# Attention projections on four column strips, with two copies moved from VectorE in a four-layer transformer kernel

## The chip, the cores and the metric

The kernel runs on one core of a Trainium2 chip. The metric is the device time of one execution in microseconds, the median of several runs. The engines of the core are named as the profile names them: PE (TensorE), PEld (TensorE's weight loads), DVE (VectorE), ACT (ScalarE), POOL (GpSimd) and SP (SyncE, which issues the transfers).

## What is computed

Sixteen sequences of 256 tokens with 256 features pass through four layers; all data is fp32. Attention has 16 heads of 16 features.

- Layer 0: norm and modulation by a condition vector, masked self attention with rotary turning of q and k, a gated residual; then cross attention to 77 context tokens with a gated residual; then an MLP (256 to 1024 to 256) with a gated residual.
- Layer 1: cross attention with biases, plain residual.
- Layer 2: self attention with biases and a gated residual, cross attention with a plain residual, MLP with a gated residual.
- Layer 3: self attention and cross attention, both with rotary turning, plain residuals; MLP.

For one attention the reference is, in short:

```
xn = norm(x) * (1 + scale) + shift
q, k, v = xn @ Wq, src @ Wk, src @ Wv        # src is xn, or the context
q, k = rope(q), rope(k)                      # layers 0 (self only) and 3
x = x + gate * (softmax(q k^T / 4 [+ mask]) v @ Wo)
```

## The kernel before

Everything stays in the core's memory: `x_sb` holds all sixteen sequences. Each batch element's attention or MLP is cut into steps. The function `add` notes a step: its engine, an assumed duration, what it depends on, which buffers it takes (`Hold`), and a priority. `Order.solve` then goes through the steps with those durations and writes the order in which every engine gets its instructions; the engines run their lists in that order and wait for each other by semaphores. The eight PSUM banks (tag `b`) are handed from step to step. Within layers 1 and 2 and within each attention stage, steps of many batch elements are interleaved; the three MLP stages stand between (roughly 630 to 860, 1612 to 1850 and 2400 to 2630 us).

PE works in several divisions of its 128 x 128 array:

- full: contraction over 128 rows (or 77, the context length) and more than 32 output columns. The projections (`project_T` L619, `rotate_tasks` L671, `mmv` L787), the output projection in `residual` (L992), the transposes (L711, L606, L498) and the MLP (L1035, L992).
- row-tiled: four groups of 32 rows side by side, each with one pair of heads: scores for the maximum (L828, L840) and scores for the exponential (L922).
- four column strips of 32: the step `values` (L945), which multiplies the exponentials by v. For each of two heads it issues four matmuls, for PSUM partitions 0, 32, 64 and 96.
- 64 x 64: the mask of layer 0, in bf16 (L915).

The planner knows them as a `kind` of step ("row", "col", or none for full) and adds a turning time of 0.2 us (0.13 for "col") where the kind changes.

An attention runs so: `norm_tasks` normalises x (POOL `xn` L491) and turns it by a DVE transpose and two transfers through DRAM (`yd`, `xr`) into `xT`, scaled by ACT (L539). The projections follow. `take_q` (ACT) writes q into `kq`. `take_k` writes k twice into `kz`, slot 0 with every other group of 16 features set to zero and slot 1 with the others (the factors are in `par`): slot 0 is ACT's (L640, L642) and slot 1 is DVE's (L644, L646). Where there is rotary turning, DVE multiplies by the tables (L683, L686), POOL adds (L691), PE transposes back (L711), and `take_q` and `take_k` read that. Scores are made, DVE takes the maxima (L854 with the mask in layer 0's self attention, L858, L862), the maxima go through DRAM back into `kq`, scores are made again with them, ACT takes exponentials into `ec` (L936, L934), `values` multiplies with v, DVE transposes (`ts` L954) and takes reciprocals (L961), POOL multiplies (`od` L967), and DVE transposes into `oT` (L971). Then `residual` multiplies by the output weights. Without a gate DVE adds the product to x (L998). With one, DVE multiplies the PSUM product by the gate `gb` into `tmp` (L1005) and POOL adds `tmp` to x (L1008).

Of the kernel before, what the change touches and what calls it, by code (L numbers as in the profile page):

```python
# [13 lines left out]
ALU = mybir.AluOpType  # L14
AX = mybir.AxisListType

B, N, D, H, HD, LC, FF = 16, 256, 256, 16, 16, 77, 1024
P = 128
# [176 lines left out]
def pixart_kernel(ctx: ExitStack, tc: tile.TileContext, x, cond_t, ctx_in, mask_c, mask_s, tables, vecs, rows,  # L195
# [28 lines left out]
    def buf(h, tag=None):  # L224

        return pools[tag or h.tag][h.no]
# [385 lines left out]
        return s, last, hc  # L612


    def project_T(dst, w, xT):

        for g in range(NC):
            for k in range(NC):
                nc.tensor.matmul(dst[:, g, :], lhsT=w[:, k, g * P:(g + 1) * P], rhs=xT[:, k, :],  # L619
                                 start=(k == 0), stop=(k == NC - 1))  # L620
# [11 lines left out]

    def take_k(s, bias, n, src, a, use, prio):

        def one(i):
            kz, sc = s["kz"], par[:, i:i + 1]
            for g in ([slice(0, NC)] if bias is None else [0, 1]):
                bi = None if bias is None else kbias[bias][:, i, g:g + 1]
                if i == 0 and bias is None:
                    nc.scalar.activation(kz[:, i], src(), AF.Copy, scale=sc)  # L640
                elif i == 0:
                    nc.scalar.activation(kz[:, i, g, :], src()[:, g, :], AF.Identity, scale=sc, bias=bi)  # L642
                elif bias is None:
                    nc.vector.tensor_scalar_mul(kz[:, i], src(), sc)  # L644
                else:
                    nc.vector.tensor_scalar(kz[:, i, g, :], src()[:, g, :], sc, bi, ALU.mult, ALU.add)  # L646
        big = n == N
        d = (0.6 if big else 0.33) if bias is None else (0.95 if big else 0.5)
        return join([add("ACT", d, lambda: one(0), deps=[a], use=use, prio=prio),
                     add("DVE", d, lambda: one(1), deps=[a], use=use, prio=prio)], prio)  # L650

    def rotate_tasks(s, key, ws, xT, src_t, n, half, uses, name, prio):


        nt = (n + P - 1) // P
        r = min(n, P)
        width = len(ws) * D
        out_t, hold = [], []
        for group in ([list(range(nt))] if len(ws) == 1 else [[t] for t in range(nt)]):
            hm, hr, hq, u = Hold("b"), Hold("rope"), Hold("qk"), {}  # L660
            nm = f"{key}_{name}_{group[0]}"
            w_all = len(group) * width

            def mm(group=group, u=u, hm=hm, hq=hq):
                u["p"] = psum(hm)
                u["r1"] = s[key, group[0]] = buf(hq)
                for i, t in enumerate(group):
                    for j, w in enumerate(ws):
                        at = (i * len(ws) + j) * D
                        for k in range(NC):  # L670
                            nc.tensor.matmul(u["p"][0:r, at:at + D], lhsT=xT()[:, k, t * P:t * P + r],  # L671
                                             rhs=w()[:, k, :], start=(k == 0), stop=(k == NC - 1))

            def turns(group=group, u=u, hr=hr):
                r1 = u["r1"]
                r2 = u["r2"] = buf(hr)
                hn = width // HD
                for i, t in enumerate(group):
                    tt = (t * P % half) // P
                    pv, v1, v2 = (a[0:r, i * width:(i + 1) * width].rearrange("q (h w) -> q h w", w=HD)  # L680
                                  for a in (u["p"], r1, r2))
                    cs = tabT[0:r, tt, 0, :].unsqueeze(1).to_broadcast([r, hn, HD])
                    nc.vector.tensor_tensor(v1, pv, cs, ALU.mult)  # L683
                    for z in range(2):
                        sn = tabT[0:r, tt, 1, 8 * z:8 * z + 8].unsqueeze(1).to_broadcast([r, hn, 8])
                        nc.vector.tensor_tensor(v2[:, :, 8 * z:8 * z + 8], pv[:, :, 8 - 8 * z:16 - 8 * z], sn,  # L686
                                                ALU.mult)

            def plus(u=u, w_all=w_all):
                r1 = u["r1"][0:r, 0:w_all]  # L690
                nc.gpsimd.tensor_tensor(r1, r1, u["r2"][0:r, 0:w_all], ALU.add)  # L691
            size = len(group) * len(ws)
            a = add("PE", size * NC * MM, mm, deps=[src_t], take=[hm, hq], use=uses, prio=prio)
            d = add("DVE", 0.75 * size, turns, deps=[a, tab_t], take=[hr], use=[hm, hq], prio=prio)
            out_t.append(add("POOL", 0.65 * size, plus, deps=[d], use=[hr, hq], prio=prio))
            hold.append(hq)
        return out_t, hold, nt, r
# [18 lines left out]
    def attention(b, name, n, wv, wkeys, h_w, w_t, eps, mod, half, biases, masked, pre_add, gate, prio, ctxs=None,  # L716
# [31 lines left out]
        if half is None:  # L748
# [6 lines left out]
            def mmk():  # L755
                p = psum(hm2)
                u["k"] = p[:, 0:NC * n].rearrange("p (c n) -> p c n", n=n)
                project_T(u["k"], wv[kk], src())
            a = add("PE", (4 * MM) if self_ else 1.0, mmk, deps=[*src_t, w_t[kk], late_t], take=[hm2], use=[h_kq, *h_src, *h_w],
                    prio=prio)  # L760
            k_t = take_k(s, bk, n, lambda: u["k"], a, [hm2, h_kq], prio)
            a = add("PE", 4 * MM, mmq, deps=[xT_t, w_t[kq], late_t], take=[hm1], use=[h_kq, hx, *h_w], prio=prio)
            q_t = take_q(s, bq, lambda: u["q"], a, [hm1, h_kq], prio)
        elif self_:
            info = rotate_tasks(s, "qk", [lambda: wv[kq], lambda: wv[kk]], lambda: s["xT"],
# [16 lines left out]
        def mmv():  # L782
            ps = uv["p"] = psum(hm3)
            xT = src()
            for t in range(nk):
                for k in range(NC):
                    nc.tensor.matmul(ps[0:rows_n, t * D:(t + 1) * D], lhsT=xT[:, k, t * P:t * P + rows_n],  # L787
                                     rhs=wv[kv][:, k, :], start=(k == 0), stop=(k == NC - 1))

        def take_v():  # L790
# [2 lines left out]
            pairs = pairs.rearrange("p t h (a w) -> p t h a w", w=HD)  # L793
            for t in range(nk):
                nc.scalar.copy(pairs[:, t, :, 0:4:3, :], pv[:, t].rearrange("p (h i) w -> p h i w", i=2))
        a = add("PE", nk * NC * MM, mmv, deps=[*src_t, w_t[kv]], take=[hm3], use=[h_v, *h_src, *h_w], prio=prio)
        v_t = add("ACT", 0.37 * nk, take_v, deps=[a, ones_t], use=[hm3, h_v], prio=prio)


# [90 lines left out]
        for g in range(NC):  # L890
            u5, avs, h_av, h_so = {}, [], Hold("b"), Hold("ts")
            for kc in range(nk):
                h_e, ex = Hold("ec"), []

                def open_e(g=g, kc=kc, h_e=h_e):
                    if g == 0 and kc == 0:
                        s["oT"] = buf(h_ot)
                    for r in range(4):
                        s["e", g, kc, r] = buf(h_e)[:, r]
                t_e = add("NO", 0.0, open_e, deps=[qx_t, v_t, barrier], take=[h_e] if g or kc else [h_e, h_ot],  # L900
                          prio=prio)
                for rp in (1, 0):
                    hs = [Hold("b"), Hold("b")]
# [66 lines left out]
            def back(g=g, u5=u5):  # L970
# [5 lines left out]


        residual(s, b, [*done, w_t[ko]], lambda k, t: s["oT"][:, k, t * P:(t + 1) * P], lambda: wv[ko], NC, [h_ot, *h_w], gate, nm,
                 prio)
        return exps  # L980


    def residual(s, b, deps, lhsT, w, nk, holds, gate, name, prio, after=None):
        hm, u = Hold("b"), {}
        xf = x_sb[:, b].rearrange("p t d -> p (t d)")
        ts = []
        for t in range(NT):
            def mm(t=t):
                if t == 0:
                    u["p"] = psum(hm, NT)  # L990
                for k in range(nk):
                    nc.tensor.matmul(u["p"][:, t, :], lhsT=lhsT(k, t), rhs=w()[:, k, :], start=(k == 0),  # L992
                                     stop=(k == nk - 1))
            ts.append(add("PE", nk * MM, mm, deps=[*deps, *ts], take=[hm] if t == 0 else [],
                          use=holds if t == 0 else [hm, *holds], prio=prio))
        if gate is None:
            def plus():
                nc.vector.tensor_tensor(x_sb[:, b], x_sb[:, b], u["p"], ALU.add)  # L998
            x_done[b] = add("DVE", 0.69, plus, deps=[*ts, x_done[b]], use=[hm], prio=prio)
            return  # L1000
        ht = Hold("tmp")

        def times():
            s["tmp"] = buf(ht)
            nc.vector.tensor_tensor(s["tmp"], u["p"], s["gb"][:, 0:1, :].to_broadcast([P, NT, D]), ALU.mult)  # L1005

        def plus():
            nc.gpsimd.tensor_tensor(xf, xf, s["tmp"].rearrange("p t d -> p (t d)"), ALU.add)  # L1008
        a = add("DVE", 0.69, times, deps=[*ts, s["gb_t"]], take=[ht], use=[hm, s["hg"]], prio=prio)
        x_done[b] = add("POOL", 1.3, plus, deps=[a, x_done[b]], use=[ht], prio=prio)  # L1010


    def mlp(b, name, wv, h_w, w_t, eps, mod, func, b1, pre_add, gate, prio, barrier, before):
# [343 lines left out]
```

## Time and profile before

| what | value |
|---|---|
| median of 3 runs | 2632.84 us (2628.79 to 2638.83) |
| the profiled execution | 2631.43 us, span 2629.7 us |
| mean granted TensorE clock | 0.995 |
| PE busy | 98% of the span, 21512 matmul records |
| DVE, ACT, POOL busy | 62%, 48%, 42% |
| DMA | 143.10 MB, mean 54 GB/s |

One fp32 matmul is two matmul records and two weight-load records. A record's own length comes from a model, and neighbours overlap, so the distance between starts is the better measure. "Line" is the line of the kernel before. In a group's line, out<-in with "32*128" gives the rows and columns of the weights. The idle time before a group is put down to what ended it.

### The profile page before, as it was taken

What the parts mean: (1) busy time and instruction counts of PE and PEld (TensorE: products, weight loads), DVE (VectorE), ACT (ScalarE), POOL (GpSimd) and SP (SyncE); (2) the same over time, 40 slices, a digit from 0 to 9 for tenths busy, and PEclk for the clock granted to TensorE, in tenths of its full rate; (3) what the DMA queues carried; (4) which work ended last, traced back from release to release, by engine and by line L of the source; (5) the groups of instructions that cost most, each with busy time, mean ns of one, the idle gap of its engine ahead of it and who ended that gap; (6) DMA issues with size and microseconds to landing.
All of it is one profiled execution on the core that took longest, in us unless ns stands there. A gap on an engine that the chain in (4) does not pass through costs nothing. (4 is left out here: it accounts for less than half of the span.)

```text
span 2629.7 us, 56144 instructions
## 1 busy us (share of the span) xinstructions
PE 2575.5 (98%) x21512; PEld 1813.2 (69%) x21512; DVE 1627.7 (62%) x4537; ACT 1255.4 (48%) x2511; POOL 1113.5 (42%) x1413
## 2 busy tenths in 40 slices
PE   8999999999999899999999999999999999999999
PEld 5555565666888666666666667888666666666888
DVE  7888886676131577777777775111888887885100
ACT  2444455664333456555556654322455555554322
POOL 5233333558452355233334656442333324657310
PEclk9999999999999899999999999999999999999999
DMA  5000101223321121111111113111100001122110
GB/s 171 30 27 29 34 25 39 73 80 101 100 78 54 40 70 54 48 55 40 39 40 38 61 62 114 64 54 45 35 28 30 28 24 37 50 66 71 56 57 29
DMA packets 159749, 143.10 MB, mean 54 GB/s; under 512 B 24648, under 2 KB 124216, under 8 KB 158712
## 3 DMA queue, kind: packets, MB, share of 16 engines
q1 hardware_dynamic: 159480, 139.51, 16.9%
q8 instruction: 169, 2.77, 0.4%
q14 instruction: 100, 0.82, 0.1%
HBM read 91.86 MB, written 47.61 MB: 53 GB/s over the span
## 5 line engine op out<-in xcount | busy, mean ns | idle before, releaser
L936 ACT ACTIVATE ec<-bank 128x512 f32<-128x512 f32 (+1 forms) x1152 | 608.5, 596 | 514.0 <-PE bank L828 260.7
L922 PE MATMUL bank<-kq 32*128 32x256 f32 (+1 forms) x5120 | 627.9, 395 | 4.8 <-DMA kq<-mrow 4.4
L491 POOL TENSOR_SCALAR xn<-x_sb,mv,rstd 128x256 f32<-128x256 f32 x320 | 451.1, 1464 | 108.4 <-DVE y L519 97.8
L922 PEld LDWEIGHTS bank<-kq 32*128 32x128 f32 (+1 forms) x5120 | 357.2, 167 | 172.8 <-issue 105.1
L828 PE MATMUL bank<-kq 32*128 32x512 f32 x1536 | 432.5, 633 | 2.4 <-ACT ec L936 2.4
L858 DVE TENSOR_REDUCE mx<-bank 128x2 f32<-128x512 f32 x544 | 341.6, 681 | 46.0 <-PE bank L828 43.7
L945 PE MATMUL bank<-ec,v 128*32 128x256 f32 (+1 forms) x5120 | 347.9, 385 | 5.8 <-ACT ec L936 3.6
L1040 ACT ACTIVATE ec<-bank,vec 128x256 f32<-128x256 f32 x384 | 159.7, 467 | 401.3 <-PE bank L1035 373.2
L1035 PE MATMUL bank<-xT,kq 128*128 128x256 f32 x1536 | 341.4, 379 | 0.0
L992 PE MATMUL bank<-kq,ec 128*128 128x256 f32 x1536 | 339.7, 379 | 0.0
L992 PEld LDWEIGHTS bank<-kq,ec 128*128 128x128 f32 x1536 | 291.5, 190 | 39.5
L1035 PEld LDWEIGHTS bank<-xT,kq 128*128 128x128 f32 x1536 | 290.5, 190 | 40.4 <-issue 1.6
L967 POOL TENSOR_TENSOR od<-ts,rec 128x128 f32<-128x128 f32 x448 | 170.1, 402 | 318.7 <-DVE rec L961 318.1
L519 DVE STREAM_TRANSPOSE y<-xn 128x512 f32<-128x512 f32 x158 | 110.9, 702 | 298.9 <-DMA yd<-y 257.6
L945 PEld LDWEIGHTS bank<-ec,v 128*32 128x32 f32 (+1 forms) x5120 | 137.2, 109 | 183.0 <-issue 75.5
L862 DVE TENSOR_REDUCE mx<-bank 128x4 f32<-128x308 f32 x512 | 211.9, 468 | 55.4 <-PE bank L922 25.3
L466 POOL TENSOR_SCALAR rstd<-mv 128x2 f32<-128x2 f32 x160 | 37.5, 235 | 423.8 <-DVE mv L461 347.7
L854 DVE CUSTOM_DVE_ANT_0 junk<-bank,ctx 128x256 f32<-128x256 f32 x448 | 188.8, 421 | 45.2 <-PE bank L828 12.2
L954 DVE STREAM_TRANSPOSE ts<-bank 128x512 f32<-128x512 f32 x224 | 158.3, 707 | 76.6 <-PE bank L945 69.1
L691 POOL TENSOR_TENSOR qk<-qk,rope 128x512 f32<-128x512 f32 (+1 forms) x96 | 112.9, 1178 | 194.4 <-DVE rope L686 151.3
L1008 POOL TENSOR_TENSOR x_sb<-x_sb,tmp 128x512 f32<-128x512 f32 x80 | 101.6, 1270 | 179.4 <-DVE tmp L1005 179.2
L840 PE MATMUL bank<-kq 32*128 32x154 f32 x2048 | 167.1, 308 | 1.5 <-DVE ts L954 0.5
(164 smaller groups left out, 3437.8 us busy)
## 6 DMA issues: line engine op xcount, KB each, us to landing
yd<-y SPq DMA_DIRECT2D x158, 256.0 KB
xr<-yd SPq DMA_DIRECT2D x158, 256.0 KB
kq<-in_mod_dram SPq DMA_DIRECT2D x10, 512.0 KB
cin<-in_ctx_in_dram SPq DMA_DIRECT2D x36, 128.0 KB
x_sb<-in_x_dram SPq DMA_DIRECT2D x16, 256.0 KB
gb<-gate_g0m SPq DMA_DIRECT2D x16, 256.0 KB
gb<-gate_g2a SPq DMA_DIRECT2D x16, 256.0 KB
gb<-gate_g2m SPq DMA_DIRECT2D x16, 256.0 KB
```

What stands on the lines that cost most here:

```text
L491: nc.gpsimd.tensor_scalar(to, of, s["mv"][:, t, 0:1], s["rstd"][:, t:t + 1], ALU.subtract, ALU.mult)
L828: ls.append(lambda ps=ps, R=R, keys=keys: nc.tensor.matmul(ps.rearrange("p (s k) -> p s k", k=N), lhsT=s["qx"][R, 0, g, t * P:(t + 1) * P] ...
L840: ls.append(lambda ps=ps, R=R, keys=keys, tt=tt: nc.tensor.matmul(ps[:, 2 * tt * n:2 * (tt + 1) * n].rearrange("p (s k) -> p s k", k=n), l ...
L854: nc.vector.tensor_tensor_reduce(junk, u[i][:, i2 * N:(i2 + 1) * N], mb[:, t, :], -1.0, 3.0e38, ALU.add, ALU.min, m[:, i2, g, t:t + 1])
L858: nc.vector.tensor_reduce(m[:, :, g, t], u[i].rearrange("p (s k) -> p s k", k=N), AX.X, ALU.max, negate=True)
L862: nc.vector.tensor_reduce(m[:, :, g].rearrange("p s t -> p t s"), u[i][:, 0:4 * n].rearrange("p (t s k) -> p t s k", s=2, k=n), AX.X, ALU. ...
L922: (lambda ps=u[i], R=R, q=q: nc.tensor.matmul(ps[0:rows_n, q * N:(q + 1) * N], lhsT=s["kz"][R, q, g, kc * P:kc * P + rows_n], rhs=s["qx"][ ...
L936: nc.scalar.activation(e, u[i][0:rows_n], AF.Exp)
L945: nc.tensor.matmul(u5["p"][32 * r:32 * r + 32, 1 - q, :], lhsT=s["v"][0:rows_n, kc, 8 * g + 2 * r + 1 - q, :], rhs=s["e", g, kc, r][0:rows ...
L967: nc.gpsimd.tensor_tensor(ov[:, :, HD * i:HD * i + HD], ts[:, i, :, HD * i:HD * i + HD], rec[:, i, :].unsqueeze(2).to_broadcast([P, N // 3 ...
L992: nc.tensor.matmul(u["p"][:, t, :], lhsT=lhsT(k, t), rhs=w()[:, k, :], start=(k == 0), stop=(k == nk - 1))
L1035: nc.tensor.matmul(u["p"][:, j, :], lhsT=wv["w1"][:, k, f * P:(f + 1) * P], rhs=s["xT"][:, k, :], start=(k == 0), stop=(k == NC - 1))
```

## The change

- A new function `strips` makes one 128-column product from four matmuls of 32 weight columns each, one for each quarter of the output's partitions, all with the same right-hand side. The self-attention projections and every q projection of 256 tokens use it, and so does the output projection of every attention (`nk == NC`). The k and v projections of the 77 context tokens, the transposes and the MLP stay as they were. The steps concerned are told to the planner as kind "col".
- In `take_k`, for 256 keys without bias (self attention of layers 0 and 3), slot 1 is also copied by ACT.
- In `residual`, for layer 0's self attention (`by_pool`), ACT copies the PSUM product into `tmp`, and POOL multiplies it by the gate and then adds it to x. The POOL step also keeps the gate buffer.
- Each step that opens an `ec` buffer also names the hold on `oT`; before, only the first did.

```diff
+    def strips(dst, pairs):
+        for k, (l, r) in enumerate(pairs):
+            for J in (slice(32 * j, 32 * j + 32) for j in range(4)):
+                nc.tensor.matmul(dst[J], lhsT=l[:, J], rhs=r, start=(k == 0), stop=(k == len(pairs) - 1))
+
+    def project_T(dst, w, xT, small=False):
         for g in range(NC):
+            if not small:
+                strips(dst[:, g, :], [(w[:, k, g * P:(g + 1) * P], xT[:, k, :]) for k in range(NC)])
+                continue
...
@@ take_k
-                if i == 0 and bias is None:
+                if bias is None and (i == 0 or big):
                     nc.scalar.activation(kz[:, i], src(), AF.Copy, scale=sc)
...
-                     add("DVE", d, lambda: one(1), deps=[a], use=use, prio=prio)], prio)
+                     add("ACT" if big and bias is None else "DVE", d, lambda: one(1), deps=[a], use=use, prio=prio)], prio)
@@ rotate_tasks
+                        if r == P:
+                            strips(u["p"][:, at:at + D], [(xT()[:, k, t * P:(t + 1) * P], w()[:, k, :]) for k in range(NC)])
+                            continue
...
-            a = add("PE", size * NC * MM, mm, deps=[src_t], take=[hm, hq], use=uses, prio=prio)
+            a = add("PE", size * NC * MM, mm, kind="col" if r == P else None, deps=[src_t], take=[hm, hq], use=uses, prio=prio)
@@ attention
-                project_T(u["k"], wv[kk], src())
+                project_T(u["k"], wv[kk], src(), not self_)
...
+                if self_:
+                    strips(ps[:, t * D:(t + 1) * D], [(xT[:, k, t * P:(t + 1) * P], wv[kv][:, k, :]) for k in range(NC)])
+                    continue
...
-                t_e = add("NO", 0.0, open_e, deps=[qx_t, v_t, barrier], take=[h_e] if g or kc else [h_e, h_ot],
+                t_e = add("NO", 0.0, open_e, deps=[qx_t, v_t, barrier], take=[h_e, h_ot],
@@ residual
+                if nk == NC:
+                    strips(u["p"][:, t, :], [(lhsT(k, t), w()[:, k, :]) for k in range(nk)])
+                    return
...
+            if by_pool:
+                nc.scalar.copy(s["tmp"], u["p"])
+            else:
+                nc.vector.tensor_tensor(s["tmp"], u["p"], s["gb"][:, 0:1, :].to_broadcast([P, NT, D]), ALU.mult)
...
+            if by_pool:
+                nc.gpsimd.tensor_tensor(s["tmp"], s["tmp"], s["gb"][:, 0:1, :].to_broadcast([P, NT, D]), ALU.mult)
             nc.gpsimd.tensor_tensor(xf, xf, s["tmp"].rearrange("p t d -> p (t d)"), ALU.add)
...
+        a = add("ACT" if by_pool else "DVE", 0.6 if by_pool else 0.69, times, deps=[*ts, s["gb_t"]], take=[ht],
+                use=[hm, s["hg"]], prio=prio)
+        x_done[b] = add("POOL", 2.6 if by_pool else 1.3, plus, deps=[a, x_done[b]], use=[ht, s["hg"]], prio=prio)
```

More of the change, by code (lines that the diff above doesn't have):

```diff
@@ L612, in context_T @@
         return s, last, hc
-    def project_T(dst, w, xT):
+    def strips(dst, pairs):
[3 more added lines that the diff above has]
+    def project_T(dst, w, xT, small=False):
         for g in range(NC):
+            if not small:
+                strips(dst[:, g, :], [(w[:, k, g * P:(g + 1) * P], xT[:, k, :]) for k in range(NC)])
+                continue
             for k in range(NC):
@@ L633, in take_k @@
     def take_k(s, bias, n, src, a, use, prio):
+        big = n == N
         def one(i):
@@ L646, in one @@
                     nc.vector.tensor_scalar(kz[:, i, g, :], src()[:, g, :], sc, bi, ALU.mult, ALU.add)
-        big = n == N
         d = (0.6 if big else 0.33) if bias is None else (0.95 if big else 0.5)
         return join([add("ACT", d, lambda: one(0), deps=[a], use=use, prio=prio),
-                     add("DVE", d, lambda: one(1), deps=[a], use=use, prio=prio)], prio)
+                     add("ACT" if big and bias is None else "DVE", d, lambda: one(1), deps=[a], use=use, prio=prio)], prio)
     def rotate_tasks(s, key, ws, xT, src_t, n, half, uses, name, prio):
@@ L757, in mmk @@
                 u["k"] = p[:, 0:NC * n].rearrange("p (c n) -> p c n", n=n)
-                project_T(u["k"], wv[kk], src())
-            a = add("PE", (4 * MM) if self_ else 1.0, mmk, deps=[*src_t, w_t[kk], late_t], take=[hm2], use=[h_kq, *h_src, *h_w],
+                project_T(u["k"], wv[kk], src(), not self_)
+            a = add("PE", (4 * MM) if self_ else 1.0, mmk, kind="col" if self_ else None, deps=[*src_t, w_t[kk], late_t], take=[hm2], use=[h_kq, *h_src, *h_w],
                     prio=prio)
             k_t = take_k(s, bk, n, lambda: u["k"], a, [hm2, h_kq], prio)
-            a = add("PE", 4 * MM, mmq, deps=[xT_t, w_t[kq], late_t], take=[hm1], use=[h_kq, hx, *h_w], prio=prio)
+            a = add("PE", 4 * MM, mmq, kind="col", deps=[xT_t, w_t[kq], late_t], take=[hm1], use=[h_kq, hx, *h_w], prio=prio)
             q_t = take_q(s, bq, lambda: u["q"], a, [hm1, h_kq], prio)
@@ L795, in take_v @@
                 nc.scalar.copy(pairs[:, t, :, 0:4:3, :], pv[:, t].rearrange("p (h i) w -> p h i w", i=2))
-        a = add("PE", nk * NC * MM, mmv, deps=[*src_t, w_t[kv]], take=[hm3], use=[h_v, *h_src, *h_w], prio=prio)
+        a = add("PE", nk * NC * MM, mmv, deps=[*src_t, w_t[kv]], take=[hm3], kind="col" if self_ else None, use=[h_v, *h_src, *h_w], prio=prio)
         v_t = add("ACT", 0.37 * nk, take_v, deps=[a, ones_t], use=[hm3, h_v], prio=prio)
@@ L895, in open_e @@
                 def open_e(g=g, kc=kc, h_e=h_e):
-                    if g == 0 and kc == 0:
-                        s["oT"] = buf(h_ot)
+                    s["oT"] = buf(h_ot)
                     for r in range(4):
                         s["e", g, kc, r] = buf(h_e)[:, r]
-                t_e = add("NO", 0.0, open_e, deps=[qx_t, v_t, barrier], take=[h_e] if g or kc else [h_e, h_ot],
+                t_e = add("NO", 0.0, open_e, deps=[qx_t, v_t, barrier], take=[h_e, h_ot],
                           prio=prio)
@@ L978, in attention, with residual @@
         residual(s, b, [*done, w_t[ko]], lambda k, t: s["oT"][:, k, t * P:(t + 1) * P], lambda: wv[ko], NC, [h_ot, *h_w], gate, nm,
-                 prio)
+                 prio, by_pool=masked and self_)
         return exps
-    def residual(s, b, deps, lhsT, w, nk, holds, gate, name, prio, after=None):
+    def residual(s, b, deps, lhsT, w, nk, holds, gate, name, prio, by_pool=False):
         hm, u = Hold("b"), {}
@@ L993, in mm @@
                                      stop=(k == nk - 1))
-            ts.append(add("PE", nk * MM, mm, deps=[*deps, *ts], take=[hm] if t == 0 else [],
+            ts.append(add("PE", nk * MM, mm, deps=[*deps, *ts], take=[hm] if t == 0 else [], kind="col" if nk == NC else None,
                           use=holds if t == 0 else [hm, *holds], prio=prio))
@@ L1004, in times @@
             s["tmp"] = buf(ht)
-            nc.vector.tensor_tensor(s["tmp"], u["p"], s["gb"][:, 0:1, :].to_broadcast([P, NT, D]), ALU.mult)
+            if by_pool:
+                nc.scalar.copy(s["tmp"], u["p"])
+            else:
+                nc.vector.tensor_tensor(s["tmp"], u["p"], s["gb"][:, 0:1, :].to_broadcast([P, NT, D]), ALU.mult)
         def plus():
+            if by_pool:
+                nc.gpsimd.tensor_tensor(s["tmp"], s["tmp"], s["gb"][:, 0:1, :].to_broadcast([P, NT, D]), ALU.mult)
             nc.gpsimd.tensor_tensor(xf, xf, s["tmp"].rearrange("p t d -> p (t d)"), ALU.add)
-        a = add("DVE", 0.69, times, deps=[*ts, s["gb_t"]], take=[ht], use=[hm, s["hg"]], prio=prio)
-        x_done[b] = add("POOL", 1.3, plus, deps=[a, x_done[b]], use=[ht], prio=prio)
+        a = add("ACT" if by_pool else "DVE", 0.6 if by_pool else 0.69, times, deps=[*ts, s["gb_t"]], take=[ht],
+                use=[hm, s["hg"]], prio=prio)
+        x_done[b] = add("POOL", 2.6 if by_pool else 1.3, plus, deps=[a, x_done[b]], use=[ht, s["hg"]], prio=prio)
     def mlp(b, name, wv, h_w, w_t, eps, mod, func, b1, pre_add, gate, prio, barrier, before):
```

## The prediction, made before the changed kernel ran

> **What bounds the kernel now.** I read the busy shares first, then the waits of PE, then PE's timeline around one projection, since the change works on PE.
>
> ```profile
> span 2629.7 us, 56144 instructions
> PE 2575.5 (98%) x21512; PEld 1813.2 (69%) x21512; DVE 1627.7 (62%) x4537; ACT 1255.4 (48%) x2511; POOL 1113.5 (42%) x1413
> DVE  7888886676131577777777775111888887885100
> ```
>
> PE is busy for all but 54 us of 2629.7. The next engine, DVE, reaches eight tenths only in the self attention of layers 0 and 3. PE's own waits are small and scattered:
>
> ```profile
> PE bank L619 <- ACT xT L539: 8.0, 1, 8.0
> PE bank L382 <- DMA kq<-in_mod_dram: 4.8, 2, 4.2
> PE bank L922 <- DMA kq<-mrow: 4.4, 3, 2.5
> ```
>
> Columns are total us, times, longest; no other waiting group of PE passes 3.6 us. So the end moves only if PE's stream becomes shorter or somebody starts to keep PE waiting. A busy PE isn't a PE at its peak, so I look inside (timeline of PE; columns: start, length, what):
>
> ```profile
> 2002.51 1.89 PE L671 MATMUL bank<-w_e,xT 128*128 128x256 f32 x8
> 2004.33 1.15 PE L922 MATMUL bank<-kq 32*128 32x256 f32 x16
> 2005.41 1.99 PE L671 MATMUL bank<-w_e,xT 128*128 128x256 f32 x8
> 2007.33 1.07 PE L945 MATMUL bank<-ec,v 128*32 128x256 f32 x16
> 2008.33 0.48 PE L922 MATMUL bank<-kq 32*128 32x256 f32 x2
> ```
>
> In the MLP, where the array's division never changes, the chain that ended last shows that a group of 32 records starts 6.91 us after the one before:
>
> ```profile
> 1701.83 6.91 PE bank L1035 x32
> 1708.73 6.91 PE bank L992 x32
> ```
>
> That is 0.216 us a record (each fp32 matmul is two records). Eight of them should take 1.73 us. The projection at 2005.41, between a row-tiled and a column-tiled group, holds PE for 2007.33 - 2005.41 = 1.92 us: **0.19 us more than its work**. The values step at 2007.33 has 16 records on four column strips; if four run at once it is four pitches, 0.864 us, and it takes 1.00: **0.14 us more**. The single instructions say where this goes. Between the last matmul start of one division and the first weight load of the next lie 307 ns instead of 216 (91 lost), and 20 more if a foursome was last, its members starting 7 ns apart. After the switch the second pass starts 322 ns after the first weight load for full and row-tiled work (106 lost, the exposed load of 128 columns), but 242 for strips (26 lost: 32 columns). These figures recur over some 200 to 350 switches of a kind.
>
> [...] Here four strips cost one pitch: the values groups repeat every 216 ns, as full matmuls do[...]
>
> **Part 1, strips.** The loops give 16 full matmuls for each batch element in each self attention (3 x 16 x 16 = 768) and 8 in each cross attention (4 x 16 x 8 = 512), together 1280: 2560 records. They become 5120 matmuls, 10240 records, in 2560 foursomes. Streaming time: 2560 pitches before, 2560 after, nothing gained. What changes is the number of switches. I count maximal stretches of one division in both kernels' instruction orders as built: full 422 before, 200 after; strips 312 before, 410 after; row-tiled and the 64-row masks hardly move (494 and 493; 127 and 128). So 222 full visits disappear; 98 remain as strip visits, and 124 have merged with a values step or another projection. A full visit costs 106 + 91 = 0.197 us, a strip visit 26 + 91 + 20 = 0.137. Gain: 222 x 0.197 - 98 x 0.137 = 43.7 - 13.4 = **30.3 us** on PE. About a quarter each falls in layers 0 and 3, half in layers 1 and 2. Merged visits are seen already: values steps of 32 records last 1.864 us, not 2 x 1.00.
>
> Added: 7680 matmul and 7680 weight-load records, and 1 MB of instructions by the count (2.77 MB now on the instruction queue for 43024 PE instructions). Row-tiled and values steps already issue eight instructions per pitch without gaps, so I price this at nothing; what covers it is the 216 ns of streaming. The new instructions wait no more often than the old: waits stand ahead of a group's first or fifth strip.
>
> **Part 2, second key slot.** DVE loses 32 x 745 ns (kq L644, 128x512) = 23.8 us; ACT gains 32 x 694 ns (L640, same shape) = 22.2. The two copies were parallel and are now in series: k is ready up to 0.69 us later, less where DVE's queue had been late. Behind them on ACT wait exponentials, which free banks and ec. ACT is half busy and each batch element has several others' work around it, so on the path: 0, with -2 to +5 us as bounds.
>
> **Part 3, gated residual of layer 0's self attention.** DVE loses 16 x 685 ns (tmp L1005) = 11.0. ACT gains 16 PSUM copies; nearest row L629, 128x512: 684 ns, 10.9 us. POOL gains 16 x 1.27 us (as L555, also a broadcast operand) = 20.3 us, 42% busy over all. x is done some 1.3 us later and the gate buffer is held 2.6 us longer; the next reader of x is that element's cross attention, sixteen elements later in the order. POOL's other work (rstd, od) can stand behind the two operations for 2.5 us; od of another element may then come late to DVE and to the output projection. On the path: 0, bounds -2 to +4. The relief of DVE in layer 0 (11.0 + 16 x 0.745 = 22.9 us in its busiest stretch) helps where the bank reducers run late; I count it in those lower bounds. The changed holding of oT moves no instruction by itself: 0.
>
> **The sum.** 2629.7 - 30.3 = 2599.4. The three other engines keep their absolute work while PE's shrinks, so some waits grow: PE waits 54 us now; I take +3 (bounds -6 to +12). That is -27 us, span 2602.7. The profiled execution took 2631.4 as a whole, near the median shown of 2632.8, so the median forecast is 2632.8 - 27.3 = **2605.5 us**. A measurement of this kernel can tell about 0.5%, 13 us, from no change.
>
> **Rivals.**
> 1. The gain is mostly eaten by waits: DVE or ACT sets the pace in the self attention of layers 0 and 3, where DVE is at 8 tenths. It needs some 20 us of new waits. Against: DVE gets 35 us lighter, and PE's waits there are a few us a stage. Time: 2622. Chance 0.09.
> 2. Strips with one shared right-hand side don't keep the pitch: the place is each of the 2560 foursomes, by issue or by reading one stream four times. At 12 ns more each (228 for 216) the gain is gone; at 17 ns it is slower by 0.5%, at 30 ns (+77 - 30) the time is 2680. For:[...] values steps read four different streams. Against: 216 ns is kept to within 1 ns in nearly all of them. Chance 0.05.
> 3. The switch gain and the relief of DVE add up, and PE's waits shrink too by 10 us: 2593. For: PE waits on oT and on reducers in layer 0 are DVE's. Chance 0.22.
> 4. The strips are not placed on separate columns and run one after another: 1280 x 3 x 0.432 = +1660 us. The output slices start at partitions 0, 32, 64, 96 just as values' do. Chance 0.01.
>
> **How the numbers follow.** The main case has 0.63, and with rival 3 makes 0.85 for faster by over 0.5%; 0.02 of rival 1 lands just beyond that bound, giving 0.87. Same: the other 0.07 of rival 1 and 0.01 of rival 2 near its break-even, 0.08. Slower: the rest of rival 2 and rival 4, 0.05. Range: main case with its bounds, -40 to -15, and rival 3's and part of rival 1's end: 2591 to 2620.
>
> **What would show it.** Right: PE groups of strips 32 x 256 with foursomes every 216 ns; 1231 stretches of one division in PE's stream instead of 1355; PE busy near 2546; the MLP stages unchanged in length; all of the difference inside attention, half of it in layers 1 and 2; DVE near 1593, ACT near 1288, POOL near 1134. Wrong: a foursome pitch over 220 ns; PE waits above 75 us; a switch into strips that costs as much as one into full.

## The result: half of the gain arrives

The changed kernel takes 2620.2 us at the median of 16 runs (2612.0 to 2629.6); the kernel before, run beside it, 2633.4. The ratio is **0.9951, interval 0.9938 to 0.9963**: some 13 us faster, not the 27 forecast. The runs of the changed kernel spread over 17 us, and the longer ones have the lower granted TensorE clock (2612.0 us at 0.995, 2629.6 at 0.988).

The page of the changed kernel, the lines that answer to those of before:

```profile
span 2617.4 us, 71563 instructions
PE 2562.5 (98%) x29192; PEld 1677.9 (64%) x29192; DVE 1596.0 (61%) x4489; ACT 1284.3 (49%) x2559; POOL 1138.9 (44%) x1429
DVE  6788886775130567777777784111878887885100
```

PE has its 7680 new matmul records and is still busy for 98%: it is idle for 54.9 us, where it was 54.2 before. DVE is 32 us lighter, ACT 29 and POOL 25 heavier. Projection and values step now stand side by side (timeline of PE: start, length, what):

```profile
2006.46 1.93 PE L619 MATMUL bank<-w_e,xT 128*32 128x256 f32 x32
2008.21 1.05 PE L960 MATMUL bank<-ec,v 128*32 128x256 f32 x16
2009.19 0.48 PE L937 MATMUL bank<-kq 32*128 32x256 f32 x2
```

From 2006.46 to 2009.19 are 2.73 us for 48 records, twelve foursomes: 12 x 0.216 + 0.137. Two groups have paid for one switch, and the foursomes keep their pitch. So the mechanism is there. What took the other half doesn't stand among PE's plain waits (total, times, longest), which are as small as before but for one:

```profile
PE bank L619 <- ACT xT L539: 8.3, 2, 7.8
PE bank L724 <- POOL qk L704: 7.9, 5, 5.4
PE bank L382 <- DMA kq<-in_mod_dram: 4.3, 3, 3.1
```

Part of it stands in the clock. The view of the cores, before and after (span, mean granted clock):

```profile
core 0: 2629.7 us, clock 0.995
```
```profile
core 0: 2617.4 us, clock 0.991
```

To see all terms I take PE's time apart, from the trace. A record is one matmul instruction in the trace, and a stretch is a row of them in one division of the array. **Stream**: each record's distance to the next at full speed (216 ns for 256 columns, 109 for 128), a quarter of it where four tiles run. **Switches**: stretches of one division times 0.197 us (full), 0.137 (strips), 0.217 (row-tiled), 0.117 (64 x 64). **Clock**: the stream time of the records that started at half speed, which they take once more. **Rest** is what remains from the start of the span to the end of the last matmul: waits, row-tiled groups out of step, and whatever the other terms leave out. The ratios and the mean clock come from repeated runs, the terms from one profiled execution each, in us.

| kernel | ratio to before (interval) | switches | clock | rest | mean clock of all timed runs |
|---|---|---|---|---|---|
| before | 1 | 248.3 | 7.5 | 174.1 | 0.9945 |
| changed | 0.9951 (0.9938 to 0.9963) | 218.3 | 16.8 | 182.7 | 0.9914 |
| strips alone, order of before | 0.9905 (0.9882 to 0.9928) | 219.2 | 10.5 | 175.0 | 0.9928 |
| full matmuls in the changed order | 1.0068 (1.0046 to 1.0090) | 248.1 | 14.5 | 190.0 | 0.9923 |
| strips, planner told | 0.9948 (0.9929 to 0.9967) | 221.0 | 13.9 | 181.1 | 0.9919 |
| moves alone, planner told | 1.0093 (1.0073 to 1.0113) | 247.7 | 20.7 | 190.7 | 0.9898 |
| moves alone, order of before | 0.9995 (0.9983 to 1.0007) | 248.3 | 6.5 | 172.0 | 0.9946 |
| all, order of before | 0.9905 (0.9889 to 0.9920) | 219.2 | 5.7 | 174.3 | 0.9940 |
| the same, gate buffer held | 0.9906 (0.9892 to 0.9921) | 219.2 | 11.1 | 175.8 | 0.9927 |
| before, delay 0.12 | 1.0119 (1.0103 to 1.0135) | 244.3 | 33.5 | 190.9 | 0.9848 |
| before, delay 0.14 | 1.0017 (1.0008 to 1.0027) | 251.8 | 10.0 | 172.7 | 0.9946 |
| before, delay 0.16 | 1.0005 (0.9997 to 1.0013) | 252.4 | 6.5 | 172.6 | 0.9950 |
| changed, delay 0.14 | 0.9945 (0.9930 to 0.9959) | 219.1 | 14.0 | 180.6 | 0.9923 |
| changed, delay 0.16 | 0.9964 (0.9952 to 0.9977) | 219.9 | 27.2 | 177.3 | 0.9872 |

The stream is 2195.8 us in all of them. Between before and changed: switches -30.0, clock +9.3, rest +8.6. The clock differs from one execution to the next (0.988 to 0.995 over the 16 of the changed kernel), so the term of one profile is rough; over the timed runs (70 of the kernel before, beside the others, and 16 of the changed one) the mean clock falls by 0.0031, and 0.0031 of 2620 us is 8 us, an estimate that agrees with the term.

### The profile page after: what moved, and what is told of

Its sections match the earlier page's. It is cut to its first block, busy times and chain, and to the rows that moved or that the text cites. A ratio compares the mean times of both kernels' runs of the same rounds, so it can differ in the third digit from the quotient of the medians.

```text
span 2617.4 us, 71563 instructions
## 1 busy us (share of the span) xinstructions
PE 2562.5 (98%) x29192; PEld 1677.9 (64%) x29192; DVE 1596.0 (61%) x4489; ACT 1284.3 (49%) x2559; POOL 1138.9 (44%) x1429
## 5 line engine op out<-in xcount | busy, mean ns | idle before, releaser
L937 PE MATMUL bank<-kq 32*128 32x256 f32 (+1 forms) x5120 | 638.3, 395 | 4.9 <-ACT ec L949 2.7
L844 PE MATMUL bank<-kq 32*128 32x512 f32 x1536 | 446.8, 634 | 1.6 <-ACT ec L951 0.8
L960 PEld LDWEIGHTS bank<-ec,v 128*32 128x32 f32 (+1 forms) x5120 | 156.4, 110 | 158.6 <-issue 39.4
L844 PEld LDWEIGHTS bank<-kq 32*128 32x128 f32 x1536 | 136.6, 183 | 40.0 <-ACT ec L951 24.6
```

Of the source, the lines that this page charges most:

```text
L844: ls.append(lambda ps=ps, R=R, keys=keys: nc.tensor.matmul(ps.rearrange("p (s k) -> p s k", k=N), lhsT=s["qx"][R, 0, g, t * P:(t + 1) * P] ...
L937: (lambda ps=u[i], R=R, q=q: nc.tensor.matmul(ps[0:rows_n, q * N:(q + 1) * N], lhsT=s["kz"][R, q, g, kc * P:kc * P + rows_n], rhs=s["qx"][ ...
L960: nc.tensor.matmul(u5["p"][32 * r:32 * r + 32, 1 - q, :], lhsT=s["v"][0:rows_n, kc, 8 * g + 2 * r + 1 - q, :], rhs=s["e", g, kc, r][0:rows ...
```

## Experiments: strips, moves and order apart

My theory after the result: the strips give what was worked out, the moves nothing, and the order that the planner writes for the new durations and engines loses some of it. The rivals: the loss comes with the strips (a shorter stream on PE leaves the clock and the other engines worse off), or with the moved copies. To tell them apart I used the planner against itself: it can be left uninformed, so that the instructions change and the order does not.

**Strips alone, in the order of the kernel before.** The changed kernel with the moves and the hold on `oT` undone, and no step told to be "col" (one of the lines concerned):

```diff
-            a = add("PE", size * NC * MM, mm, kind="col" if r == P else None, deps=[src_t], ...
+            a = add("PE", size * NC * MM, mm, deps=[src_t], ...
```

> The kernel before with the 1280 projections cut into strips and nothing else; the planner is not told, so every engine keeps the order of the kernel before. The stretches of one division in PE's order give switches of 218.5 us against 247.9. Theory (switches shorten PE by 30 us; what is lost again is TensorE clock and waits): PE's switching falls by 29 us in the trace. If the loss comes with the strips themselves[...], this one too gains only 12 to 16 us and its mean granted clock is about 0.991 to 0.993 against about 0.995. If the loss comes from the moved copies and the new order, it gains 24 to 29 us at the clock of the kernel before.

Measured: 2609.1 us, ratio 0.9905. The strips gain 25 us where the order stays, so the first rival doesn't explain the missing half. It has a small share: the switches fall by 29 us, and the mean clock of the three kernels with strips in this order is 0.993 over 17 runs, against 0.9945 before, which is some 3 to 4 us of lost clock.

**Full matmuls in the changed order.**

```diff
-            for J in (slice(32 * j, 32 * j + 32) for j in range(4)):
-                nc.tensor.matmul(dst[J], lhsT=l[:, J], rhs=r, ...
+            nc.tensor.matmul(dst, lhsT=l, rhs=r, ...
```

> The changed kernel, same order on every engine, but each projection as one full matmul again. Theory (clock and waits come with the new order and the moved copies): slower than before by 5 to 15 us, since the loss is there without the gain, with a clock below 0.995. Rival (the loss belongs to the strips): within 4 us of the kernel before, and at its clock.

Measured: 2653.0 us, ratio 1.0068: 18 us slower than before, more than expected. At this order too, the strips are worth 1.2% (0.9951 against 1.0068).

**Strips with the planner told; the moves alone with the planner told.** The first keeps slot 1 and the gate on VectorE, the second has no strips and no "col". Both have the changed hold on `oT`.

> The kernel before with strips, with the planner told, and the holding of oT as changed; slot 1 of the keys and the gate stay on VectorE. If the two moves cost the missing time: 24 to 30 us faster than before. If they cost nothing: like the changed kernel, 11 to 16 us faster.

> The kernel before with slot 1 of layers 0 and 3 on ScalarE, the gate of layer 0 by ScalarE and GpSimd, and the holding of oT; no strips. If the moves cost the missing time: 8 to 15 us slower than before. If they cost nothing on the path: within 5 us of before.

Measured: 0.9948 and 1.0093. Told of the strips, the planner gives away 11 us of the 25; told of the moves, it loses 25 us, more than I expected. The two losses don't add up: with both told, the changed kernel stands at 0.9951, as with the strips alone. This can't say yet whether the moves themselves or their order cost the time.

**The moves in the order of before, alone and with the strips.** Only the emission is moved; the planner still counts them as VectorE's:

```diff
-                     add("ACT" if big and bias is None else "DVE", d, lambda: one(1), ...
+                     add("DVE", d, lambda: one(1), ...
-        a = add("ACT" if by_pool else "DVE", 0.6 if by_pool else 0.69, times, ...
+        a = add("DVE", 0.69, times, ...
```

In these two the gate's buffer is given on when VectorE would have been done with it, so GpSimd may multiply by a later element's gate.

> The two moves alone (key slot 1 of layers 0 and 3 on ScalarE, layer 0's gate by ScalarE copy and GpSimd product), planned as if they were still on VectorE, so that every engine's order is that of the kernel before; no strips. Theory (the moves themselves are off the path, the new order costs the time): within 5 us of before. Rival (ScalarE's two copies in series and the longer GpSimd step delay PE wherever they stand): 12 to 25 us slower than before, as with the moves in their own order.

> Strips and both moves, in the order of the kernel before. Theory (strips give 25 us, moves nothing, the new order takes 10 to 20): 22 to 28 us faster than before, some 10 us faster than the changed kernel. Rival (moves cost): 5 to 14 us faster than before.

Measured: 0.9995 and 0.9905. The moves cost nothing on the path, and the second rival falls: with the instructions of the changed kernel and the order of the kernel before the gain is 25 us. The version in which GpSimd's step keeps the gate buffer confirms it:

```diff
-        x_done[b] = add("POOL", 1.3, plus, deps=[a, x_done[b]], use=[ht], prio=prio)
+        x_done[b] = add("POOL", 1.3, plus, deps=[a, x_done[b]], use=[ht, s["hg"]], prio=prio)
```

> Strips and both moves in the order of the kernel before, as in the run with all in the old order, and with the gate buffer held until GpSimd has used it. PE's order is that of the kernel before. If the order is what costs: again 22 to 28 us faster than before, 10 to 16 us faster than the changed kernel. If the longer hold of the gate buffer matters: between the two.

Measured: 2607.7 us, 0.9906. It computes all that the changed kernel computes and beats both kernels. Against the strips alone (0.9905) it differs by the moves, which add and cost nothing.

**How much an order is worth.** One constant of the planner, the delay that it assumes between engines, redraws every order:

```diff
-    LAG = 0.13
+    LAG = 0.14        # also 0.12 and 0.16
```

> The kernel before with one planning constant, the assumed delay between engines, at 0.14 for 0.13 us: the same instructions on the same engines in another order, with switches of 251.4 us for 247.9. If the kernel before has an order that is lucky against its neighbours, this is 8 to 25 us slower, with more clock loss and waits. If order hardly matters: within 5 us (3.5 of them switches).

> The changed kernel with the same constant at 0.14: another order of the same instructions, switches 218.3 for 217.5 us. If the changed kernel's order is an ordinary draw, within 12 us of it on either side; if order hardly matters, within 4 us.

> The kernel before with the planner's delay at 0.12 for 0.13: another order of the same work, planned switches 243.9 us for 247.9. If redrawn orders are as a rule worse than the one the kernel before has: 4 to 20 us slower in spite of 4 us fewer switches. If order costs only its switches: 1 to 7 us faster.

> The same with 0.16: planned switches 251.9 us, and in layer 3 clearly other pairs of row-tiled steps. If redrawn orders are as a rule worse: 8 to 25 us slower. If order costs only its switches: 2 to 7 us slower.

> The changed kernel with 0.16: planned switches 219.2 us for 217.5. If its order is an ordinary draw: within 12 us of it on either side; if order costs only its switches: 0 to 4 us slower.

Measured, for the kernel before: +0.2% at 0.14, +1.2% at 0.12, nothing at 0.16. The 32 us at 0.12 lie beyond both expectations, and at 0.16 the 1 us lies just below both. For the changed kernel: 0.9945 at 0.14 and 0.9964 at 0.16, around its 0.9951. So "redrawn orders are as a rule worse" doesn't hold: 0.16 has 4 us more switches and other pairs in layer 3, and is as fast as before. What holds is that an order can cost anything from nothing to 32 us, that its count of switches doesn't tell which (0.12 has the fewest), and that the changed kernel's three orders cost 10 to 16 us, measured against the same work in the order of before.

## Experiments: why the clock drops

The worst order, at 0.12, loses 33.5 us to the clock by the table; here its view of the cores:

```profile
core 0: 2668.4 us, clock 0.984
```

In the changed kernel, one drop looks like this (timeline of PE, idle time before it in brackets):

```profile
499.92 2.43 PE L382 MATMUL bank<-condT,kq 128*128 128x16 f32 x16 [0.40 <-DMA kq<-in_mod_dram]
502.28 1.94 PE L960 MATMUL bank<-ec,v 77*32 77x256 f32 x16
503.99 3.64 PE L619 MATMUL bank<-w_a,oT 128*32 128x256 f32 x32
507.56 0.64 PE L937 MATMUL bank<-kq 32*77 32x256 f32 x2
```

The values step takes 1.94 us for 1.05, the strips 3.64 for 1.93. In the view of stretches (busy us of PE, PEld, DVE, ACT, POOL; granted clock; DMA):

```profile
497.80:501.20 3.40, 3.00 (x46) 2.11 (x34) 2.40 (x7) 2.22 (x3) 0.76 (x2) 1.00 0.49 169
501.20:508.00 6.80, 6.80 (x60) 3.67 (x63) 2.84 (x11) 0.00 (x0) 3.56 (x6) 0.50 0.04 10
```

PE was busy for 3.00 of the 3.40 us ahead of the drop. But the modulation step L382 multiplies 16 columns for every load of 128 weight columns, so the array does little. To put a number on it I counted the time in which columns stream (216 ns for 256), weighted by the share of the array's rows and columns in use: an estimate from the records of the two profiles, before and changed. They show twelve half-speed stretches ahead of the program's end, from 3.4 to 10.2 us long. In the 3.4 us ahead of each, the array streamed 0.23 of what it could at the median; over the whole of both profiles, cut into pieces of that length, the median is 0.86. PE was busy for 0.54 of the time ahead at the median, and for 0.88 and 0.93 of it ahead of the two at 501 and 911 us. So PE waits ahead of most of these drops, but it needn't have been idle for the clock to fall. How little must stream, and for how long, these runs don't show.

To test whether the little streaming counts, I made that step multiply more in the same time. The 16 columns are repeated six times. The records start every 112 ns with 16 columns and with 96, so the columns don't set the pace (what does was not shown), and the step grows by only 0.05 to 0.07 us from its start to the start of what follows:

```diff
-                        nc.tensor.matmul(s["ps"][:, 2 * i + c, :], ..., rhs=c_t[:, k, :], ...
+                        nc.tensor.matmul(wide[:, 2 * i + c], ..., rhs=c_t[:, k, :].unsqueeze(1).to_broadcast([P, 6, B]), ...
```

> The changed kernel, same order; only the ten modulation steps (L382) multiply with 96 right-hand columns, the 16 of the condition six times over, instead of 16. [...] they take as long as before, but the array multiplies six times as much in that time. Theory[...]: the half-speed stretches at 501 and 911 us, each right behind such a step, are gone, those at 583, 614, 624 and 2365 stay; the clock term falls by 4 to 7 us; 2613 to 2616 us. Rival (the clock answers to waiting only, or to the strips): both stretches stay, within 2 us of the changed kernel.

> The same widening in the kernel before ordered with the delay of 0.12, which runs at a clock of 0.984 and was 32 us slower than before. Three of its half-speed stretches (506 for 13.7 us, 899 for 13.7, 939 for 10.2) stand right behind a modulation step. Theory: those at 506 and 939 go or shorten, the one at 899, behind 8 us of waiting, stays; 5 to 11 us faster than without the widening, so 21 to 27 us slower than before. Rival: within 3 us of 32 slower.

> The widening in the version with all of the change in the order of the kernel before, which was 25 us faster than before. One short stretch at 907 us stands behind a modulation step and one of 20 us at 866 behind it and a long wait. Theory: 0 to 5 us more, 25 to 31 us faster than before. Rival: no difference beyond 2 us.

Measured for the changed kernel: 2613.2 us, ratio 0.9931 (0.9918 to 0.9943), against 0.9951 without the widening: 5 us. The intervals touch, but the mean clock rises from 0.9914 (16 runs) to 0.9942 (5 runs), and the clock term falls from 16.8 to 11.7 us. The same place in its timeline:

```profile
499.19 2.00 PE L383 MATMUL bank<-condT,kq 128*128 128x96 f32 x16 [0.20 <-DVE rec L977]
501.11 1.07 PE L961 MATMUL bank<-ec,v 77*32 77x256 f32 x16
502.00 1.91 PE L620 MATMUL bank<-w_a,oT 128*32 128x256 f32 x32
```

The stretch at 501 is gone, and so is the one at 911; of the others only some stayed, and two short new ones appeared near 1558 and 1586, so their places are not fixed from one profile to another, and these two prove little.

For the order of 0.12 the proof is better: 1.0087 (1.0071 to 1.0102) against 1.0119, 8 us, with a mean clock of 0.9900 for 0.9848, a clock term of 23.6 us for 33.5, and its stretches at 506 and 939 gone. At the first of these two PE's wait and step lie alike in both profiles. Without and with the widening (the step in the timeline, then the view of stretches for the 3.4 us around it and the 3.4 us after):

```profile
503.92 1.93 PE L382 MATMUL bank<-condT,kq 128*128 128x16 f32 x16 [1.94 <-DMA kq<-in_mod_dram]
502.50:505.90 3.40, 1.98 (x20) 1.98 (x24) 0.62 (x2) 0.00 (x0) 1.26 (x1) 1.00 0.23 81
505.90:509.30 3.40, 3.40 (x36) 1.91 (x35) 1.59 (x6) 0.00 (x0) 0.46 (x2) 0.51 0.57 154
```
```profile
502.02 2.00 PE L383 MATMUL bank<-condT,kq 128*128 128x96 f32 x16 [2.02 <-DMA kq<-in_mod_dram]
500.50:503.90 3.40, 1.88 (x16) 1.86 (x16) 0.63 (x2) 0.00 (x0) 1.26 (x1) 1.00 0.23 81
503.90:507.30 3.40, 3.40 (x58) 2.33 (x57) 2.64 (x9) 1.17 (x3) 0.76 (x2) 1.00 0.54 154
```

PE waits as long (2.02 us for 1.94) and is busy no longer (1.88 for 1.98), but in the 3.4 us around the step the array streamed 0.38 of what it could instead of 0.09, an estimate by the same count, and the clock after it is 1.00 instead of 0.51. So it isn't the waiting alone. That kernel has no column-cut projection at all, so the drop isn't the strips' either. For the best version: 0.9908 (0.9892 to 0.9923), no difference from 0.9906, which fits theory and rival alike; it had little to win there.

## Why the prediction was wrong, point by point

- **Switches as the price: right.** Forecast -30.3 us, in the trace 248.3 to 218.3, -30.0. Stage by stage too: layers 1 and 2 (from the end of the first MLP to the last output projection of layer 2) took 753.0 us and take 738.0, their switches 87.3 and 72.6; half of the gain, 15 us, was forecast there. In the order of the kernel before, the whole forecast holds: 25 us for 27.
- **The pitch of strips: right.** 216 ns with one shared right-hand side. Rivals 2 and 4 fall.
- **Moves at nothing on the path: right** (0.9995 in the order of before; 0.9951 with and 0.9948 without them where the planner is told of the strips), with sizes slightly off: DVE lost 31.7 us for 34.8, ACT gained 28.9 for 33.1 (the PSUM copy of the gate takes 575 ns, where I took 684 from L629, and the two slot copies in a row overlap by 112 to 152 ns: together they add 18.7 us for 22.2), POOL 25.4 for 20.3, though the product itself takes 20.3. Rival 3 falls with them: the relief of DVE brings nothing.
- **"So the end moves only if PE's stream becomes shorter or somebody starts to keep PE waiting": this step failed.** The sum had two places for time, switches and waits, and priced all else of the new order with "some waits grow; I take +3". The waits it meant came out about so: PE's idle time grew by 0.7 us. But time was lost while PE was busy: the rest grew by 8.6 us and, as the next point says, the clock term by 9.3.
- **Where the rest grew.** Layer 3's attention alone (from layer 2's MLP to the next) has +13.7, from 43.1 to 56.8, and layer 0 -5.4. With strips in the order of before layer 3's rest is 42.6, and in the new orders of the strips alone and the moves alone it is 49.2 and 58.8, so it goes with the order. In layer 3 the four row tiles are out of step more often: with each record counted as 216 ns for 256 columns from its start, one of four multiplies alone for 26.0 us instead of 15.0, two for 42.0 instead of 40.1, three for 25.0 instead of 18.8, which is (11.0 x 3 + 1.9 x 2 + 6.2) / 4 = 11 us of array time. A wait of 5.4 us for POOL's rotary addition is new there, but PE's idle time in this stage grows by only 2 us.
- **The clock had no term: this failed as well.** +9.3 us. I had the mean clock 0.995 on the page and read it as constant. Clock and rest together are 18 where the sum had 3.
- **The range was added wrongly.** The bounds of the terms (waits -6 to +12, second slot -2 to +5, gate -2 to +4) with -30.3 give -40 to -9, not -40 to -15. That would have reached to 2624, but without naming the cause.
- **Rival 1** had nearly the right size, 20 us of new losses for 18, and the wrong cause: it named DVE or ACT as the pace, but VectorE lighter or heavier made no difference at the same order.
- Of what was to show it, the stretches came (1235 in the trace, 1231 forecast), and so did the busy times of DVE, ACT and POOL within 5 us. PE's busy time did not: 2562.5 us for 2546.

Open is what in the new order puts layer 3's row tiles out of step. The holding of oT, which the versions in the order of before leave as it was, was not run by itself.

## What to carry to other kernels

Where a planner writes the order from durations and engines, a change of one step is a change of every engine's order: price the work at a fixed order first, and then let the planner be told, because the two may differ by as much as the gain. On an engine that is busy all the time look for switches between divisions of the array, which the busy share hides. And count the columns that the array streams in each few microseconds, not its busy time: a wait together with small matmuls behind large weight loads halved the clock for what followed here (0.50 over 6.80 us).

## What the hardware showed that I had not expected

- Four column strips with the same right-hand side keep the pitch of one full matmul, 216 ns for 256 fp32 columns, over 32 records and more in a row (a group of 32 takes 1.864 us with its switch).
- The granted clock fell to 0.50 for 6.8 us although PE had been busy for 3.00 of the 3.40 us before; a step of 16 records with only 16 columns each had begun there. At a drop in the order of 0.12, with 96 columns in place of 16 the clock was 1.00 instead of 0.51, though PE waited as long (2.02 us for 1.94).
- Widening a matmul from 16 to 96 columns kept the pace of 112 ns a record (the step grew by 0.05 to 0.07 us of 1.7 to 1.9) and made two kernels 5 and 8 us faster; a third, which had little clock to win, stayed as it was.
